# Two ways to end a gated-experts kernel: tails for the whole last unit, or pairs and rows closed inside it

## The chip, the cores and the metric

The kernel runs on one core of a Trainium2 chip. The metric is the device time of one execution in microseconds (us); lower is better. A core has TensorE (matrix products, into the PSUM banks), VectorE, ScalarE and GpSimd (called PE, DVE, ACT and POOL in the profile), and SyncE (SP), which issues most of the transfers (DMAs).

## What is computed

`x` holds 8 items of 512 positions by 256 channels, all in float32. Eight experts and a shared one have weights of 256 by 1024 (gate, up) and 1024 by 256 (down).

```python
g = einsum('bsd,edf->ebsf', h, Wg)
u = einsum('bsd,edf->ebsf', h, Wu)
expert_outs = einsum('ebsf,efd->ebsd', silu(g) * u, Wd)
expert_output = einsum('be,ebsd->bsd', gating_probs, expert_outs)
shared = einsum('bsf,fd->bsd', silu(h @ Sg) * (h @ Su), Sd)
sg = shared_gate_prob[:, :, None]
out = x + (1.0 - sg) * expert_output + sg * shared
```

## The kernel before

The work is cut into 36 **units**: two halves of four items, nine experts, and two groups of four blocks of 128 hidden columns. A unit multiplies four items j by four blocks i, gate and up (m = 0 and 1), which gives sixteen tiles h[i, j] of 128 by 512, and multiplies these with the down weights. Both products are done with fewer multiplications than the plain ones, by sums and differences of operands: the diagonal i = j first (the *hub*: `P_step`, `Q_step`), then six **pairs** (i, j) of `PAIRS` (line 66), each with the two off-diagonal tiles (`R1_step`, `R_step`, lines 534 to 553). One "product" here is 128x128 by 128x512 and shows as two matmul records in the profile.

Each bank goes the same way. For r = 1 VectorE adds D (line 552); for m = 0 ScalarE applies Silu (line 477); for m = 1 VectorE multiplies gate, coefficient and up into h (line 482). Before a pair, ScalarE **seeds** a bank by copying an earlier difference into it (line 532), and the pair's product accumulates on that. The operands of a pair are V and b (sums of x) and U and W (sums of weights); in unit 0 they are computed (`x_difference` line 319, `x_sums` lines 334 and 335, `w_difference` 417, `w_sums` 427 to 430) and V, b are stored to DRAM, from where later units load them (lines 324, 341).

The **down projection** of a unit is `down` (line 587), 26 products, run while the next products of gate and up are running: it starts at the unit's step 22 (`TAKE`) and ends in the next unit. Per pair there are three products: `first` (r), `second` (S or s) and the product of X = h[j, i] - h[i, j] (line 674). Then for each i come p_i (sums of rows, with accumulator b_i) and q_i (sums of columns, with accumulator B_i). GpSimd makes the row and column sums (line 577). The accumulators stay in SBUF over all units of a half; `carried` copies one into a bank with ScalarE (line 615), multiplies, and copies it back (line 624); `put` adds a bank to an accumulator with VectorE (lines 603 to 607). There are two banks for all this (`new_po`), used in turn.

A half must be **closed** (`closes`): in its last unit each pair adds its accumulator V to the bank (line 678) and puts the sum into b_i and b_j, and each row i puts p_i into B_i. The closed b_i and B_i are a transposed output.

The order on TensorE and GpSimd is written by hand and is the program's order; ScalarE's too in unit 0. It comes from strings (lines 874 to 878): G is one step of gate and up, D one of down, T one of turning x, X one tail. On the other queues the framework's scheduler puts the instructions in order; `issue_after` (line 123) makes one instruction stand behind another in its queue, without a semaphore. `BEHIND` (line 300) is a table of such pairs for unit 0.

The **last unit** (n = 35) is different. Its down projection is not done by pairs: each of its 32 `tail` steps (line 763) multiplies a half of h[i, j] with the plain down weights, four records of 128x128 by 128x256, straight into rows of the output. So the accumulators of the second half are closed one unit earlier, in unit 34, whose down ends in the hub of unit 35. There `END_STEPS` (line 886) lists, by the number of G steps done: "turn" transposes b_i and B_i of a row (line 739), "store" sends them in eight DMAs to a DRAM scratch (issued at line 953, one for each G), "load" brings them back as rows in two DMAs (line 757), "x" loads the rows of x, "add" adds both on GpSimd (line 761). When a tail group is complete, `store_rows` (line 775) adds it to those rows on VectorE and stores them to the output.

Of the kernel before, what the change touches and what calls it, by code (L numbers as in the profile page):

```python
# [17 lines left out]
def kernel(  # L18
# [40 lines left out]
    P = 128  # L59
# [5 lines left out]
    CI = (0.0, 1.0, -1.0, 2.0)  # L65
    PAIRS = ((1, 0), (0, 2), (3, 0), (1, 2), (3, 1), (3, 2))

    OWN = (0, 1, 2, 3)
# [71 lines left out]
    xdram = {}  # L140
    recent = {}


# [152 lines left out]
    def load_x(h, i):  # L296
# [4 lines left out]
        ("b", 0): ("x", 2), ("v", 1): ("P", 2), ("h", 2): ("P", 3), ("v", 2): ("other", 0, 1),  # L301
        ("b", 1): ("v", 2), ("h", 3): ("v", 2), ("v", 3): ("X", 0), ("v", 4): ("X", 1), ("v", 5): ("X", 2),
    }
# [170 lines left out]
    def finish(u, m, i, j, bank):  # L474
        if m == 0:
            s = spool.tile([P, S], F32, tag="sg", name=f"sg{i}{j}_{u.name}")
            nc.scalar.activation(s, bank, AF.Silu)  # L477
            u.sg[i, j] = s
        else:
            b = NI * u.h + j  # L480
            t = hpool.tile([P, S], F32, tag="h", name=f"h{i}{j}_{u.name}")
            made = ve.scalar_tensor_tensor(  # L482
                t, u.sg[i, j], coef[:, u.e, b : b + 1], bank, ALU.mult, ALU.mult
            )
            if i == j:
                first_order(u, made, "h", i)
            u.h_[i, j] = t
# [56 lines left out]
    def R_step(u, p, m, r):  # L544
        i, j = PAIRS[p] if r == 0 else PAIRS[p][::-1]
        bank = u.bank[i, j, m]
        nc.tensor.matmul(  # L547
            bank, u.W[p][:, r, m], u.VB[p][:, r],
            start=False, stop=True, skip_group_check=True,
        )  # L550
        if r == 1:
            ve.tensor_add(bank, bank, u.Ds[j, m])  # L552
        finish(u, m, i, j, bank)


    def h_sums(u, p):


        i, j = PAIRS[p]
        if u.n + 1 == len(units):  # L560
            return
        u.X[p] = tpool.tile([P, S], F32, tag="t", name=f"X{p}_{u.name}")
        made = (gp if closes(u) and p in (1, 2, 3, 4) else ve).tensor_tensor(  # L563
            u.X[p], u.h_[j, i], u.h_[i, j], ALU.subtract
        )
        first_order(u, made, "X", p)
        for k, l in ((i, j), (j, i)):
            for which, n in (("rows", k), ("cols", l)):
                u.sums.append((which, n, (k, l)))
# [12 lines left out]

    def closes(u):

        return u.n + (2 if u.h + 1 == NH else 1) == len(units) * (u.h + 1) // NH

    def down(u, acc):
# [54 lines left out]
        def pair(p):  # L642
# [8 lines left out]
            def second():  # L651
                args = u.Wd[p][j], u.h_[j, i]
                if p in OWN and not closes(u):
                    carried(("S", p), *args)
                    return
# [8 lines left out]

            if closes(u) and p < SWAPPED:
                second()
                yield
                A, k = first()
            else:
                A, k = first()  # L670
                yield
                second()
# [3 lines left out]
            )  # L676
            if closes(u):
                ve.tensor_add(A, A, acc["V", p])
                put(("b", i), A, 1.0 / d)
                put(("b", j), A, -1.0 / d)  # L680
            else:
                put(("V", p), A, 1.0)
# [4 lines left out]
        done = {}  # L687
        for what in (0, 1, 2, 3, 4, "p0", "q0", 5, "q1", "p1", "q2", "p2", "q3", "p3"):
            if isinstance(what, int):
# [14 lines left out]
            else:  # L704
# [3 lines left out]
                done[what] = po  # L708
            if closes(u) and f"p{i}" in done and f"q{i}" in done:
                if CI[i] != 0.0:  # L710
# [7 lines left out]
    def turn_back(h, i, r):  # L718
# [5 lines left out]
        if (i, 1 - r) not in BACK[BACK.index((i, r)):]:  # L724
            for q in range(4):
                outgoing.append((squares(out, NI * h + i, q), t[ts(q, 32)]))

    last_rows = {}
    tails = {}
    ended = {}  # L730
    end_rows = {}

    def end_step(kind, i):

        b = NI * (NH - 1) + i
        if kind == "turn":
            t = iopool.tile([P, 2, S], F32, tag="io", name=f"end{i}")
            for r in range(2):
                ve.transpose(t[:, r], ends.pop((NH - 1, i, r)))
            ended[i] = t  # L740
        elif kind == "store":
            to = end_rows[i] = dram.tile([S, D], F32, tag=f"end{i}", name=f"endrows{i}")
            at = to.rearrange("(c r t) d -> r t c d", r=32, t=NT)
            for r in range(2):
                for q in range(4):
                    outgoing.append((
                        at[:, :, :, ts(4 * r + q, 32)],
                        ended[i][ts(q, 32), r].rearrange("r (t c d) -> r t c d", t=NT, d=32),
                    ))
        elif kind == "x":  # L750
            last_rows[i] = load_rows(xpool, "x", b)
        elif kind == "load":
            at = end_rows[i].rearrange("(p t) d -> p t d", t=NT)
            end_rows[i] = []
            for c in range(2):
                t = sumpool.tile([P, 2, D], F32, tag="sum", name=f"endin{i}_{c}")
                nc.sync.dma_start(t, at[:, 2 * c : 2 * c + 2])
                end_rows[i].append(t)
# [4 lines left out]
    def tail(u, i, j, c):  # L763

        first = (j, c) not in tails
        if first:
            pool, tag = (ps_g, f"g{c}") if j == 2 else (ps_o, f"po{c}")
            tails[j, c] = pool.tile([P, 2, D], F32, tag=tag, name=f"tail{j}_{c}")
# [6 lines left out]
    def store_rows(j, c):  # L775
        b = NI * (NH - 1) + j
        xr = last_rows[j][c]
        for t in (0, 1) if j == NI - 1 and c == 1 else (slice(0, 2),):
            ve.tensor_add(xr[:, t], tails[j, c][:, t], xr[:, t])
            at = out[b].rearrange("(p c t) d -> p c t d", c=2, t=2)[:, c]  # L780
            nc.sync.dma_start(at[:, t], xr[:, t])

# [8 lines left out]
    def gate_up(u, nxt):  # L791
# [5 lines left out]
        def sums(p):  # L797
            x_sums(u, p)
            w_sums(u, p)

        for p, make in ((0, w_difference), (0, w_sums), (1, w_difference), (1, w_sums)):
            make(u, p)
        if u.n:
            make_at(u, 3)
        w_difference(u, 2)
        ahead = ((0, x_difference), (0, x_sums), (1, x_difference), (1, x_sums), (2, x_difference))
        if u.n:
# [3 lines left out]
        for kind, i, m in hub_steps(u):  # L811
# [17 lines left out]
            at = range(10, 16) if u.n in LATE_FORMS else range(3, 14, 2)  # L829
            if step == at[0] - 1 and u.n and nxt is not None:  # L830
                make_ad(u)
            if step in at and u.n and nxt is not None:
                d_forms(u, at.index(step))
            yield
        if u.n == 0:
            make_ad(u)
            for p in range(len(PAIRS)):
                d_forms(u, p)
        for p in range(len(PAIRS)):
            last = p + 1 == len(PAIRS)  # L840
            if p + 3 < len(PAIRS):
                (differences if u.n else partial(w_difference, u))(p + 3)
            if nxt is not None:
                if p >= 2:
                    load_w(nxt, p - 2)
                    if p < 5:
                        make_at(nxt, p - 2)
            store_forms(u)
            if p == 5 and nxt is not None:
                load_d(nxt)  # L850
            if not last and u.n:
                seed(u, p + 1)
            for m in range(2):
                if not last and (u.n or p or m):
                    R1_step(u, p + 1, m)
                elif last and nxt is not None:
# [3 lines left out]
                for r in range(2):  # L860
                    R_step(u, p, m, r)
                    if m == 1 and r == 1:
                        h_sums(u, p)
                        if u.n == 0 and p + 2 < len(PAIRS):
                            seed(u, p + 2)
                        if p + 2 < len(PAIRS):
                            sums(p + 2)
                        if u.n == 0 and p < 2:
                            x_difference(u, p + 3)
                    if u.n == 0 and (p, m, r) == (3, 0, 1):  # L870
                        x_difference(u, 5)
# [5 lines left out]
    FIRST = "TGGTGGTGG" + "G" * 16 + BLOCK * 5  # L877
    LAST = HUB + BLOCK + "GGXGGXGGX" * 5 + "X" * 17
    TAILS = [
        tuple(int(n) for n in what)  # L880
        for what in (
            "000 100 001 101 200 201 300 301 110 111 010 011 210 211 310 311 "
            "220 020 120 221 021 121 330 030 130 331 031 131 320 321 230 231"
        ).split()
    ]
    END_STEPS = {
        7: (("turn", 0), ("store", 0)), 16: (("turn", 1), ("store", 1)), 18: (("x", 0),),
        20: (("turn", 2), ("store", 2), ("x", 1)), 22: (("load", 0), ("x", 2)),
        24: (("turn", 3), ("store", 3), ("x", 3)), 28: (("add", 0),), 30: (("load", 1),),
        34: (("add", 1),), 37: (("load", 2),), 40: (("add", 2),), 44: (("load", 3),),  # L890
        47: (("add", 3),),
    }

    for i in range(NI):
# [37 lines left out]
    for u in units:  # L932
# [6 lines left out]
        for what in FIRST if u.n == 0 else LAST if nxt is None else ORDER:  # L939
            if what == "G":  # L940
                if nG == TAKE:
                    for _ in behind:
                        pass
                    if u.opens:
                        acc = {}
                    behind = down(u, acc) if nxt is not None else iter(())
                if final and nxt is not None and nG in (18, 21, 24, 27):
                    load_x(u.h + 1, (nG - 18) // 3)
                if nxt is None:
                    for what_, i in END_STEPS.get(nG, ()):  # L950
                        end_step(what_, i)
                if outgoing:
                    nc.sync.dma_start(*outgoing.pop(0))
                if nG > TAKE and nG % 2 == 0 and u.sums:
                    add_sum(u)
# [5 lines left out]
            elif what == "T":  # L961
                for _ in range(2):
                    next(turning, None)
            elif what == "X":
                i, j, c = TAILS.pop(0)
                tail(u, i, j, c)
# [56 lines left out]
```

## Time and profile before

| | |
|---|---|
| median of 3 runs | 2434.99 us (2433.91 to 2435.68) |
| the profiled execution | 2433.26 us, span 2431.5 us, TensorE's clock 1.000 |
| TensorE busy in the first 20 us, the next 20, the last 11.5 | 18.51, 19.44, 7.70 us |
| TensorE's waits, by releaser | 1.2 us for a memset at the start, 0.8 for ScalarE's seed (line 532, twice), 0.3 for VectorE (line 208) |
| SP's waits for VectorE's finished rows (line 781) | 26.1 us, 7 times |
| tails (line 770) | 128 records, 379 ns each |

A line of the timeline reads: start in us from the beginning of the span, duration, engine, line, operation, what it writes <- what it reads (tile names without numbers), shape, and how many records were merged; in brackets the idle time before it and what released it. Matmul records overlap: the busy time of one is 592 ns, but the next starts before it ends, so the distance between starts is what counts. A row of DMA issues ends with the size of one and the median time from issue to landing.

### The profile page before, as it was taken

Reading aid. Unit: us, or ns where it says so; the run is one execution under the profiler, and the core shown is the slowest. Engines: PE = TensorE matmul, PEld = TensorE weight load, DVE = VectorE, ACT = ScalarE, POOL = GpSimd, SP = SyncE. Lnnn points to the kernel's source line nnn. Section 1 sums busy time; section 2 is a strip of 40 time slices with the busy share of each in tenths; the row PEclk is TensorE's granted clock in tenths of the full one; section 3 lists DMA queues with packets and bytes.
Section 4 is the critical chain, followed back from the end, with each engine's and each line's share of the span. In section 5 each row is a group of like instructions: output and inputs, shape, how many; then the busy total and the mean of one; then the engine's idle time right before and its main releaser. Section 6 shows DMA issues by size and latency. Waiting matters only on the chain.

```text
span 2431.5 us, 22779 instructions
## 1 busy us (share of the span) xinstructions
PE 2425.3 (100%) x5736; PEld 1085.0 (45%) x5736; DVE 1918.3 (79%) x2861; ACT 1240.0 (51%) x2294; POOL 2085.3 (86%) x2321
## 2 busy tenths in 40 slices
PE   9999999999999999999999999999999999999999
PEld 4444444444444444444444444444444444444446
DVE  7788878778787877787887777777877777777795
ACT  5555454554555555555455555555455555555542
POOL 8988888898988989898888888888888888888882
PEclk9999999999999999999999999999999999999999
DMA  4333333334333333334353323323333333233245
GB/s 150 114 110 111 107 95 103 119 117 125 105 120 105 101 113 94 109 113 124 119 122 112 91 83 91 92 87 90 100 104 104 95 99 91 87 89 93 83 133 140
DMA packets 221201, 257.92 MB, mean 106 GB/s; under 512 B 64016, under 2 KB 156432, under 8 KB 221072
## 3 DMA queue, kind: packets, MB, share of 16 engines
q1 hardware_dynamic: 220240, 256.17, 35.7%
q8 instruction: 48, 0.79, 0.1%
q14 instruction: 81, 0.66, 0.1%
q10 hardware_dynamic: 832, 0.30, 0.0%
HBM read 238.59 MB, written 17.83 MB: 105 GB/s over the span
## 4 chain that ended last, share of the span: by engine, by line
PE 99%; DVE 1%; issue 0%; ACT 0%; DVEq 0%
PE c L547 30%; PE c L537 15%; PE c L515 10%; PE c L493 10%; PE r L639 7%; PE r L674 7%; PE b L616 5%; PE S L616 5%; PE q L639 5%; PE s L639 2%; PE tail L770 1%; PE B L616 0%; DVE h L482 0%; DVE c L542 0%; DVE c L552 0%
## 5 line engine op out<-in xcount | busy, mean ns | idle before, releaser
L547 PE MATMUL c<-b,wb 128*128 128x512 f32 x1728 | 847.2, 592 | 0.0
L477 ACT ACTIVATE sg<-c 128x512 f32<-128x512 f32 x576 | 343.8, 597 | 574.4 <-DVE c L552 332.4
L482 DVE SCALAR_TENSOR_TENSOR h<-sg,coef,c 128x512 f32<-128x512 f32 x576 | 427.4, 742 | 242.2 <-PE c L547 134.8
L547 PEld LDWEIGHTS c<-b,wb 128*128 128x128 f32 x1728 | 328.2, 190 | 409.2 <-issue 388.7
L537 PE MATMUL c<-v,u 128*128 128x512 f32 x864 | 441.1, 593 | 0.8 <-ACT c L532 0.8
L577 POOL TENSOR_TENSOR rows<-rows,h 128x512 f32<-128x512 f32 x280 | 369.3, 1319 | 0.0
L542 DVE TENSOR_TENSOR c<-D,c 128x512 f32<-128x512 f32 x432 | 298.7, 692 | 78.1 <-ACT sg L477 59.3
L577 POOL TENSOR_TENSOR cols<-cols,h 128x512 f32<-128x512 f32 x280 | 358.4, 1280 | 0.0
L552 DVE TENSOR_TENSOR c<-c,D 128x512 f32<-128x512 f32 x432 | 298.5, 691 | 21.2 <-PE c L547 20.7
L493 PE MATMUL c<-x,w 128*128 128x512 f32 x572 | 274.5, 592 | 0.0
L429 POOL TENSOR_TENSOR wb<-u,wb 128x256 f32<-128x256 f32 x108 | 78.8, 730 | 221.4 <-ACT wb L427 221.4
L537 PEld LDWEIGHTS c<-v,u 128*128 128x128 f32 x864 | 163.4, 190 | 207.9 <-issue 167.7
L674 PE MATMUL r<-X,ud 128*128 128x512 f32 x420 | 214.5, 592 | 0.0
L639 PE MATMUL r<-h,wd 128*128 128x512 f32 x420 | 214.5, 592 | 0.0
L515 PE MATMUL c<-x,at 128*128 128x512 f32 x432 | 208.5, 592 | 0.0
L525 ACT COPY D<-c 128x512 f32<-128x512 f32 x284 | 165.7, 584 | 81.4 <-DVE h L482 81.3
L563 DVE TENSOR_TENSOR X<-h,h 128x512 f32<-128x512 f32 x202 | 198.1, 981 | 6.8
L577 POOL TENSOR_TENSOR rows<-h,h 128x512 f32<-128x512 f32 x140 | 195.1, 1394 | 0.0
L577 POOL TENSOR_TENSOR cols<-h,h 128x512 f32<-128x512 f32 x140 | 180.6, 1290 | 0.0
L499 ACT COPY P<-c 128x512 f32<-128x512 f32 x216 | 126.4, 587 | 106.1 <-PE c L493 101.5
L493 PEld LDWEIGHTS c<-x,w 128*128 128x128 f32 x572 | 108.5, 190 | 135.9 <-issue 111.7
L615 ACT COPY S<-accS 128x512 f32<-128x512 f32 x132 | 77.8, 590 | 157.5 <-DVE accV L603 140.7
(115 smaller groups left out, 3473.6 us busy)
## 6 DMA issues: line engine op xcount, KB each, us to landing
b<-xs SPq DMA_DIRECT2D x210, 512.0 KB, 3.6
v<-xs SPq DMA_DIRECT2D x210, 256.0 KB, 2.6
wd<-in_L_cond_Wd_dram SPq DMA_DIRECT2D x32, 512.0 KB, 4.9
w<-in_L_cond_Wg_dram SPq DMA_DIRECT2D x127, 128.0 KB, 3.5
w<-in_L_cond_Wu_dram SPq DMA_DIRECT2D x127, 128.0 KB, 3.6
f<-xd SPq DMA_DIRECT2D x12, 512.0 KB, 5.2
xs<-f SPq DMA_DIRECT2D x18, 256.0 KB, 2.9
xin<-in_x_dram SPq DMA_DIRECT2D x16, 256.0 KB, 4.4
```

What stands on the lines that cost most here:

```text
L477: nc.scalar.activation(s, bank, AF.Silu)
L482: made = ve.scalar_tensor_tensor(t, u.sg[i, j], coef[:, u.e, b : b + 1], bank, ALU.mult, ALU.mult)
L493: nc.tensor.matmul(bank, u.raw[i][:, m, 0], xhub[u.h, i][:, 0], start=True, stop=True)
L515: nc.tensor.matmul(bank, u.at[i][:, m], xhub[u.h, i][:, 1], start=False, stop=True, skip_group_check=True,)
L537: nc.tensor.matmul(bank, u.U[p][:, m], u.V[p], start=False, stop=True, skip_group_check=True)
L542: first_order(u, ve.tensor_sub(other, u.Ds[j, m], bank), "other", p, m)
L547: nc.tensor.matmul(bank, u.W[p][:, r, m], u.VB[p][:, r], start=False, stop=True, skip_group_check=True,)
L552: ve.tensor_add(bank, bank, u.Ds[j, m])
L577: gp.tensor_tensor(sums[n], u.h_[n, n] if first else sums[n], u.h_[at], ALU.add)
L616: nc.tensor.matmul(po, w, b, start=not full, stop=True, skip_group_check=full)
L639: nc.tensor.matmul(po, w, b, start=True, stop=True)
L674: nc.tensor.matmul(A, u.Ud[p], u.X[p], start=False, stop=True, skip_group_check=True)
```

## The change

In the last unit, pairs 0, 1 and 3 of `PAIRS`, which are (1, 0), (0, 2) and (1, 2), are kept as pairs with their three down products each, and rows 0, 1 and 2 get their p and q. These pairs and rows are closed in unit 35; pairs 2, 4, 5 and row 3 are closed in unit 34 as before. Only the tails with a 3 in them stay, 14 of 32. The pairs of the last unit run in the order 0, 1, 3, 2, 4, 5. Its string is written anew, so are `TAILS` and `END_STEPS`; rows 1 and 2 get their last steps when twelve tails are left, with `issue_after` for each group of stores and loads. Six of the eight stores of row 2 go to ScalarE's queue, its transposed tiles come from another pool.

Besides, five places of the order of issue: in unit 0 the sum b of pair 1 and the second bank of pair 1 stand behind the add (line 552) of pair 0, `w_sums` comes before `x_sums`, and `x_difference` of pair 5 comes one step earlier; in closings the add of V (line 678) stands behind the h that was made last.

```diff
+    LAST_PAIRS = (0, 1, 3)
+    LAST_ROWS = (0, 1, 2)
...
-        ("b", 1): ("v", 2), ("h", 3): ("v", 2), ("v", 3): ("X", 0), ("v", 4): ("X", 1), ("v", 5): ("X", 2),
+        ("b", 1): ("add", 0, 0), ("other", 1, 0): ("add", 0, 0), ("h", 3): ("v", 2), ("v", 3): ("X", 0), ("v", 4): ("X", 1), ("v", 5): ("X", 2),
...
-            nc.scalar.activation(s, bank, AF.Silu)
+            u.last_silu = nc.scalar.activation(s, bank, AF.Silu)
...
+            latest_h[:] = u, made
...
-            ve.tensor_add(bank, bank, u.Ds[j, m])
+            first_order(u, ve.tensor_add(bank, bank, u.Ds[j, m]), "add", p, m)
...
-        if u.n + 1 == len(units):
+        if p not in pairs_of(u):
             return
...
+    def closes(u, p=None, i=None):
+
+        if u.h + 1 < NH:
+            return u.closes
+        if (p in LAST_PAIRS) if i is None else (i in LAST_ROWS):
+            return is_last(u)
+        return u.n + 2 == len(units)
...
-            if closes(u):
-                ve.tensor_add(A, A, acc["V", p])
+            if closes(u, p):
+                made = ve.tensor_add(A, A, acc["V", p])
+                if latest_h[0] is u:
+                    issue_after(made, latest_h[1])
                 put(("b", i), A, 1.0 / d)
                 put(("b", j), A, -1.0 / d)
...
-        for what in (0, 1, 2, 3, 4, "p0", "q0", 5, "q1", "p1", "q2", "p2", "q3", "p3"):
+        order = (0, 1, 2, 3, 4, "p0", "q0", 5, "q1", "p1", "q2", "p2", "q3", "p3")
+        for what in (0, 1, "p0", "q0", 3, "q1", "p1", "q2", "p2") if is_last(u) else order:
...
+                    queue = nc.scalar if i == 2 and 4 * r + q < 6 else nc.sync
...
+                if i in LAST_ROWS:
+                    issue_after(made, recent["b"])
+                latest_rows[:] = [made]
+                if i in (1, 2):
+                    issue_after(made, closing_stores[2, nc.sync][-1])
...
-            x_sums(u, p)
-            w_sums(u, p)
-
+            for make in (x_sums, w_sums) if u.n else (w_sums, x_sums):
+                make(u, p)
...
-                    if u.n == 0 and (p, m, r) == (3, 0, 1):
+                    if u.n == 0 and (p, m, r) == (3, 0, 0):
                         x_difference(u, 5)
...
-    LAST = HUB + BLOCK + "GGXGGXGGX" * 5 + "X" * 17
+    LAST = HUB + BLOCK * 3 + "GDGDGGDGDGD" + "GDDGDDGGGG" + "GGGXGGGXX" + "X" * 11
...
-            "000 100 001 101 200 201 300 301 110 111 010 011 210 211 310 311 "
-            "220 020 120 221 021 121 330 030 130 331 031 131 320 321 230 231"
+            "330 331 030 031 300 301 310 311 130 131 230 231 320 321"
...
+        18: (("x", 0),), 20: (("x", 1),), 22: (("x", 2),),
+        24: (("turn", 3), ("store", 3), ("x", 3)), 34: (("load", 3),),
+        39: (("turn", 0), ("store", 0)), 42: (("turn", 1), ("store", 1)),
+        43: (("turn", 2), ("store", 2), ("load", 0)), 46: (("add", 3), ("add", 0)),
     }
+    LAST_STEPS = (("load", 1), ("load", 2), ("add", 1), ("add", 2))
...
+                if len(TAILS) == 12:
+                    for made in closing_stores[0, nc.sync][4:]:
+                        issue_after(made, recent["b"])
+                    for made in closing_stores[1, nc.sync]:
+                        issue_after(made, *latest_rows)
+                    for made in closing_stores[2, nc.scalar]:
+                        issue_after(made, u.last_silu)
+                    for made in closing_stores[2, nc.sync]:
+                        issue_after(made, *closing_stores[1, nc.sync])
+                    for what_, i in LAST_STEPS:
+                        end_step(what_, i)
```

## The prediction

> **What bounds the kernel now.** I read the page first: busy shares and the chain that ended last.
>
> ```profile
> PE 2425.3 (100%) x5736; PEld 1085.0 (45%) x5736; DVE 1918.3 (79%) x2861; ACT 1240.0 (51%) x2294; POOL 2085.3 (86%) x2321
> PE 99%; DVE 1%; issue 0%; ACT 0%; DVEq 0%
> ```
>
> TensorE is the bound from the first product to the last, at a granted clock of 1.000. Only two things can change the time: the number of products, and holes in TensorE's row. So I looked for holes in the timeline of TensorE. One 128x128 by 128x512 product is two matmul records; their starts lie 0.43 us apart, so a product is 0.86 us of pace. In the first unit the pace breaks at three places:
>
> ```profile
> 27.98 1.88 PE L547 MATMUL c<-b,wb 128*128 128x512 f32 x4
> 30.40 1.13 PE L537 MATMUL c<-v,u 128*128 128x512 f32 x2 [0.54 <-ACT c L532]
> ...
> 38.23 1.02 PE L537 MATMUL c<-v,u 128*128 128x512 f32 x2
> 39.27 1.12 PE L547 MATMUL c<-b,wb 128*128 128x512 f32 x2
> ...
> 53.11 1.02 PE L674 MATMUL r<-X,ud 128*128 128x512 f32 x2
> 54.42 1.10 PE L537 MATMUL c<-v,u 128*128 128x512 f32 x2 [0.30 <-ACT c L532]
> ```
>
> Four records from 27.98 should hand over at 29.70; the next starts at 30.40. After each hole the following record is another 0.1 late. The holes are 0.8, 0.3 and 0.5 us. The next are in the closing of each half. This is the second half's:
>
> ```profile
> 2315.14 1.02 PE L674 MATMUL r<-X,ud 128*128 128x512 f32 x2
> 2316.00 1.02 PE L537 MATMUL c<-v,u 128*128 128x512 f32 x2
> 2316.86 1.02 PE L547 MATMUL c<-b,wb 128*128 128x512 f32 x2
> 2317.93 1.12 PE L616 MATMUL S<-h,wd 128*128 128x512 f32 x2
> ```
>
> The S product should start at 2317.72. VectorE over the same time says why it waits:
>
> ```profile
> 2316.54 0.69 DVE L678 TENSOR_TENSOR r<-r,accV 128x512 f32<-128x512 f32 x1
> 2317.14 0.73 DVE L482 SCALAR_TENSOR_TENSOR h<-sg,coef,c 128x512 f32<-128x512 f32 x1
> 2317.79 0.68 DVE L603 TENSOR_TENSOR accb<-r,accb 128x512 f32<-128x512 f32 x1
> ```
>
> The closing add stands ahead of the h that S reads; h ends at 2317.87. The hole is 0.2 plus 0.1 us, and the first half has the same one at 1178.5 to 1179.1. Both halves show another 0.3 us in the next unit's hub (1227 to 1229, 2366 to 2368). Everything between is full: 1000.00 us busy in a window of 1000 us.
>
> Then the end:
>
> ```profile
> 2425.93 3.16 SPq L781 DMA_DIRECT2D out_dram<-xin  x5
> 2427.80 0.76 DVE L779 TENSOR_TENSOR xin<-tail,xin 128x256 f32<-128x256 f32 x2 [0.17 <-PE tail L770]
> ```
>
> TensorE's last record starts at 2427.32; the additions and the last store take the span to 2431.5. The profiled run is 2433.26 us, 1.73 below the median of the runs, 2434.99.
>
> **Part 1, fewer products.** Before, the last unit's down projection is 32 tail steps, each four 128x256 records, 0.86 us. After, 14 tails stay, and the three kept pairs add 3 x 3 products, their three rows and three columns 6. 14 + 15 = 29, three products less: 3 x 0.86 = **2.6 us**, all on the bound engine.
>
> **Part 2, the first unit.** Hole 1: ScalarE's seed copy (29.76) follows a Silu (29.13) that waited for VectorE's add at L552 (28.41). TensorE finished that add's product by 27.3, but VectorE ran the sum b of pair 1 (27.02, 0.87) and another bank (27.81, 0.68) first. Both go behind the add now, which can start at 27.32; the seed ends at 29.2 and the hole is gone. What is late next: VectorE runs without a break from 23.9 to 35.2, and the reorder takes no work off it. Its v of pair 3 (33.47 to 34.68) starts a chain of six ScalarE instructions up to the seed that ends at 37.78; TensorE asks for that seed at 38.23 before and would ask at 37.4 after. So of 0.8 us about 0.35 survive. Hole 2: the product at 39.27 waits for POOL's L429, 38.49 to 39.22, behind a 1.27 us POOL sum at 37.26. With weights first, L429 ends at 37.99; POOL's sum comes 1.45 us later, ends at 40.0, and is read by the product at 40.5. The hole closes (0.3). Hole 3: ScalarE at 52.20 runs Silu, then a multiply of v (0.5), then a copy, then the seed. The multiply goes ahead of the Silu, into 1.2 us of its idle time, so the seed ends about 0.5 earlier; VectorE's 0.26 us of waiting at 44.5 gives some too. Total after the third hole: between 0.35 (the waits only move) and 1.6 (all three close); I take **0.9**, the sum of what VectorE's unbroken stretch lets through.
>
> **Part 3, the closing add behind h.** The S product no longer waits in the first half: 0.3 us. In the second half pairs 0 and 1 don't close there any more, which leaves ordinary order: 0.3 us. Behind the add stand two updates of accumulators, 0.6 us each, whose readers come products later. Total **0.6**. The holes in the hubs stay: they are Silu, copy and seed behind one product, and nothing edits that.
>
> **Part 4, what the last unit must now close.** Here the change adds waits, and TensorE's order is written by hand, so it blocks. Product p0 is seeded from accumulator b0, and b0 gets its last term from X of pair 1, with one product (0.86) between X and p0. The path from X: h (0.65, now forced ahead), closing add (0.6), b0 (0.6), ScalarE's copy (0.6), p0. The nearest row is the old closing of pair 5: X starts at 2359.23, the copy it releases ends at 2363.66, 4.43 us, with a foreign add (0.75) and a second accumulator (0.6) in it. Less these, 3.1, and with h ahead 3.7; X and one product cover 1.72. Stall: 1.4 to 2.0, I take 1.8. Product p1 comes two products after X of pair 3 and reuses the bank in which X was summed, so both accumulators must be written first: by counting 4.0, by the row 4.43, less 2.58 covered: 1.5 to 1.9, and 3.1 should the transposes of row 0 get ahead on VectorE; I take 1.6, near the row. Queued behind these on TensorE is everything that remains; nothing takes it back. Below nothing isn't possible for either: the sum before had no such pair of products and no hole there. Sum **+3.4**. ScalarE (51%) and POOL have room: POOL idles 9.76 us at 2366 and 5.70 at 2378, and takes on 12 sums of 1.3, two X and the forms of three pairs.
>
> **Part 5, the rows at the end.** Rows 0, 1, 2 are now turned, stored, loaded and added behind p2. From the end of p2 there are 22 products, 18.9 us. The longest way is row 2: six of its eight stores wait on ScalarE's queue for the last Silu, six products later, 6.7 us with its add; then six issues. The rows for these are:
>
> ```profile
> endrows<-end SPq DMA_DIRECT2D x32, 64.0 KB, 3.1
> endin<-endrows SPq DMA_DIRECT2D x8, 256.0 KB, 4.0
> ```
>
> An issue is 0.616 (median of the 32), so the stores are out at 10.4 and landed at 13.5; load issue 0.4, landing 4.0 at the median, 3.55 for the last one before, where it is quiet; then two POOL additions of 1.27. That ends at 19.5 to 20.0; the last product is ready at 19.1. The Trainium skill ("DMA: Bandwidth & Descriptors", [...]Issuing engines are not separate DMA queues) says that a second queue saves only the time to initiate, "usually small relative to the DMA itself". Here the issue row, six times 0.62, is as long as a landing, so on SP these would cost 3.7 us more; but on ScalarE they also wait for the Silu. I keep to the rows: **+0.4**, with 0 by the shortest landings (2.1, 3.0) and +3 by the longest (4.6, 4.7).
>
> **Sum:** -2.6 - 0.9 - 0.6 + 3.4 + 0.4 = -0.3. 2433.26 - 0.3 = 2433.0 for a profiled run; on the median, 2434.99 - 0.3 = **2434.7**. About 0.2% (4.9 us) is what a measurement of this kernel can tell from no change: 2430.1 to 2439.9.
>
> **Rivals.** *The saving is kept*: the seeds of p0 and p1 come in time because VectorE reached its adds early, and the end is hidden: -2.6 - 0.9 - 0.6 = -4.1, 2430.9; with all first-unit holes closed 2430.2. For it: VectorE has gaps of 0.4 to 1.9 us in the last unit before. Against: p0 hangs on a path of four dependent instructions that one product can't cover. *The closing ends late*, the slower side: SP takes row 0's eight stores, load 0, row 1's eight stores and the loads one behind the other, each load standing until its stores land. By the rows, load 1 goes out 12 us after p2 if VectorE turns row 0 six us before p2. VectorE has 24 us of work in the 23 us from X of pair 1 on (11.5 for the banks and h of three pairs, 14 accumulator updates at 0.6, six transposes at 0.67). From 4 us of lateness on, load 1 lands at 20, POOL's four additions (5.1) follow, and the end is some 6 us behind TensorE: -0.7 + 6 = 2440.3. *The first unit only moves its waits* and hubs or pairs gain nothing: -2.6 - 0.6 + 3.8 + 0.4, 2436.
>
> **How the numbers follow.** Forecast (2433 to 2437) 0.58; saving kept (2430.2 to 2433) 0.25; waits moved 0.07; late closing 0.10. Faster by over 0.2% needs everything: 0.04. Slower is the late closing nearly whole: 0.09. Same 0.87. The range leaves out the end of each rival: 2431 to 2438.
>
> **What would show it.** TensorE with 5694 records (5736 - 128 + 14 x 4 + 15 x 2). No hole at 29.7 and 39.1, a smaller one near 37.4 or 53. No S hole at 1178 and 2317. In the last unit a hole of 1.5 to 2 us ahead of a b product (L616), twice. At the end, POOL's last addition within 1 us of TensorE's last product. If there is no hole in the last unit, part 4 is wrong; if the last additions wait for a load by several us, part 5 is.

## The result, and the profile after

The changed kernel is slower. Its median is 2445.19 us (2442.23 to 2447.68, 6 runs), against 2435.34 for the kernel before, run beside it: +9.9 us, a ratio of 1.0038 (95% interval 1.0028 to 1.0049). The range on record, 2431 to 2438, does not hold it.

The profiled run took 2443.51 us, 10.25 more than the profiled run of before, with 5694 matmul records, as forecast. The page's busy shares and chain:

```profile
PE 2426.4 (99%) x5694; PEld 1077.6 (44%) x5694; DVE 1926.5 (79%) x2873; ACT 1246.2 (51%) x2306; POOL 2105.1 (86%) x2344
PE 96%; DVE 2%; POOL 1%; issue 0%; ACT 0%; DMA 0%; ACTq 0%; POOLq 0%; DVEq 0%; SPq 0%
```

TensorE is busy 1.1 us longer with 42 records fewer, and the chain leaves it for 4% of the span instead of 1%: the time went into holes. (Line numbers are those of the changed kernel: L552 was L547, L542 was L537, L633 was L616, L691 was L674, L557 was L552, L656 was L639, L486 was L482, L582 was L577.) The timeline of TensorE in the first unit:

```profile
28.10 1.88 PE L552 MATMUL c<-b,wb 128*128 128x512 f32 x4
29.81 1.02 PE L542 MATMUL c<-v,u 128*128 128x512 f32 x2
...
36.68 1.06 PE L691 MATMUL r<-X,ud 128*128 128x512 f32 x2
38.18 1.10 PE L542 MATMUL c<-v,u 128*128 128x512 f32 x2 [0.43 <-ACT c L537]
39.11 1.02 PE L552 MATMUL c<-b,wb 128*128 128x512 f32 x2
...
52.84 1.02 PE L691 MATMUL r<-X,ud 128*128 128x512 f32 x2
54.12 1.10 PE L542 MATMUL c<-v,u 128*128 128x512 f32 x2 [0.25 <-ACT c L537]
```

The hole at 29.7 is gone (29.81 follows 28.10 at the pace). It came back one pair later, at 38.18, as the prediction said it might; the one at 39.1 closed, the one at 53.7 stayed at 0.4. In unit 35, the last, TensorE's timeline shows what made most of the loss:

```profile
2366.00 1.96 PE L520 MATMUL c<-x,at 128*128 128x512 f32 x4
2369.80 1.13 PE L656 MATMUL q<-cols,ad 128*128 128x512 f32 x2 [1.84 <-POOL cols L582]
...
2383.64 1.88 PE L552 MATMUL c<-b,wb 128*128 128x512 f32 x4
2386.48 1.13 PE L691 MATMUL r<-X,ud 128*128 128x512 f32 x2 [0.96 <-ACT sg L481]
...
2395.47 1.02 PE L542 MATMUL c<-v,u 128*128 128x512 f32 x2
2398.85 2.04 PE L633 MATMUL b<-rows,wd 128*128 128x512 f32 x2 [2.37 <-ACT b L632]
2400.69 1.64 PE L552 MATMUL c<-b,wb 128*128 128x512 f32 x2
...
2410.28 1.02 PE L656 MATMUL q<-cols,ad 128*128 128x512 f32 x2
2413.90 1.12 PE L633 MATMUL b<-rows,wd 128*128 128x512 f32 x2 [2.60 <-ACT b L632]
```

The b products at 2398.85 and 2413.90 are p0 and p1. Summing what every distance between two starts has beyond the pace gives, in us (the numbers in the table are these sums, not the idle times in brackets):

| hole | before | after |
|---|---|---|
| first unit | 1.8 | 1.5 |
| closing of the first half | 0.65 | 0.63 |
| unit 34 | 0.3 | 1.25 |
| unit 35: hub, q waits for GpSimd | 0.3 | 2.2 |
| unit 35: X of pair 0, X of pair 3 | - | 1.5, 0.4 |
| unit 35: p0, then four records at half speed | - | 2.5, 1.6 |
| unit 35: p1, p2 | - | 2.9, 0.6 |

That is 12.0 us more; three products less give 2.6 back; TensorE's last record starts at 2436.76 instead of 2427.32 (+9.4). The span ends 4.9 us behind that start instead of 4.2 (+0.8). Together 10.2.

### The profile page after: what moved, and what is told of

The parts are those of the page before. It is cut to its first block, busy times and chain, and to the rows that moved or that the text cites. A ratio compares the mean times of both kernels' runs of the same rounds, so it can differ in the third digit from the quotient of the medians.

```text
span 2441.7 us, 22735 instructions
## 1 busy us (share of the span) xinstructions
PE 2426.4 (99%) x5694; PEld 1077.6 (44%) x5694; DVE 1926.5 (79%) x2873; ACT 1246.2 (51%) x2306; POOL 2105.1 (86%) x2344
## 4 chain that ended last, share of the span: by engine, by line
PE 96%; DVE 2%; POOL 1%; issue 0%; ACT 0%; DMA 0%; ACTq 0%; POOLq 0%; DVEq 0%; SPq 0%
PE c L552 29%; PE c L542 15%; PE c L520 10%; PE c L498 10%; PE r L656 7%; PE r L691 7%; PE b L633 5%; PE S L633 5%; PE q L656 5%; PE s L656 2%; DVE h L486 0%; DVE c L557 0%; POOL cols L582 0%; POOL rows L582 0%; PE B L633 0%
## 5 line engine op out<-in xcount | busy, mean ns | idle before, releaser
L552 PE MATMUL c<-b,wb 128*128 128x512 f32 x1728 | 847.6, 593 | 0.0
L486 DVE SCALAR_TENSOR_TENSOR h<-sg,coef,c 128x512 f32<-128x512 f32 x576 | 427.2, 742 | 241.2 <-PE c L552 130.8
L552 PEld LDWEIGHTS c<-b,wb 128*128 128x128 f32 x1728 | 328.6, 190 | 413.6 <-issue 393.7
L542 PE MATMUL c<-v,u 128*128 128x512 f32 x864 | 441.1, 593 | 0.7 <-ACT c L537 0.7
L582 POOL TENSOR_TENSOR rows<-rows,h 128x512 f32<-128x512 f32 x283 | 373.1, 1318 | 0.0
L582 POOL TENSOR_TENSOR cols<-cols,h 128x512 f32<-128x512 f32 x283 | 361.8, 1278 | 0.0
L547 DVE TENSOR_TENSOR c<-D,c 128x512 f32<-128x512 f32 x432 | 298.5, 692 | 78.7 <-ACT sg L481 59.5
L557 DVE TENSOR_TENSOR c<-c,D 128x512 f32<-128x512 f32 x432 | 298.4, 691 | 18.8 <-PE c L552 18.5
L542 PEld LDWEIGHTS c<-v,u 128*128 128x128 f32 x864 | 163.5, 190 | 209.0 <-issue 166.4
L691 PE MATMUL r<-X,ud 128*128 128x512 f32 x426 | 217.8, 593 | 1.1 <-ACT sg L481 1.0
L656 PE MATMUL r<-h,wd 128*128 128x512 f32 x426 | 217.7, 592 | 0.0
L582 POOL TENSOR_TENSOR rows<-h,h 128x512 f32<-128x512 f32 x143 | 198.9, 1391 | 0.0
L582 POOL TENSOR_TENSOR cols<-h,h 128x512 f32<-128x512 f32 x143 | 184.6, 1291 | 0.0
```

The source lines that it names most:

```text
L486: made = ve.scalar_tensor_tensor(t, u.sg[i, j], coef[:, u.e, b : b + 1], bank, ALU.mult, ALU.mult)
L542: nc.tensor.matmul(bank, u.U[p][:, m], u.V[p], start=False, stop=True, skip_group_check=True)
L547: first_order(u, ve.tensor_sub(other, u.Ds[j, m], bank), "other", p, m)
L552: nc.tensor.matmul(bank, u.W[p][:, r, m], u.VB[p][:, r], start=False, stop=True, skip_group_check=True,)
L557: first_order(u, ve.tensor_add(bank, bank, u.Ds[j, m]), "add", p, m)
L582: gp.tensor_tensor(sums[n], u.h_[n, n] if first else sums[n], u.h_[at], ALU.add)
```

## The experiments

**Theory:** TensorE's order, written by hand, asks for products of unit 35 before VectorE, ScalarE or GpSimd can have fed them. **Rivals:** the rows' way to the end (turn, store, load, add) sets the time; or the first-unit edits cost it. Medians, with the kernel before run beside each set:

| run | median us | before | ratio (95%) |
|---|---|---|---|
| e1, the five places alone | 2434.42 | 2435.54 | 0.9995 (0.9987 to 1.0004) |
| e12, the same again | 2434.02 | 2435.42 | 0.9994 (0.9985 to 1.0002) |
| e2, late forms | 2443.28 | 2435.54 | 1.0029 (1.0017 to 1.0040) |
| e3, p not seeded | 2444.12 | 2435.54 | 1.0033 (1.0021 to 1.0046) |
| e4, row 3 turned later | 2444.84 | 2435.54 | 1.0039 (1.0027 to 1.0052) |
| e5, e2 and pair 3 ahead of p0 | 2441.98 | 2435.24 | 1.0026 (1.0015 to 1.0037) |
| e6, e5 with loads behind all stores | 2442.16 | 2435.24 | 1.0027 (1.0018 to 1.0036) |
| e7, e6 with a shared addition and stores 4 and 4 | 2444.84 | 2435.24 | 1.0036 (1.0024 to 1.0049) |
| e8, row 2 on one queue | 2444.33 | 2436.14 | 1.0035 (1.0022 to 1.0049) |
| e9, no way for rows 0 to 2 | 2446.34 | 2436.14 | 1.0043 (1.0030 to 1.0056) |
| e10, e5 without that way | 2436.83 | 2436.14 | 1.0005 (0.9997 to 1.0013) |
| e11, e5 with another order on SyncE | 2441.56 | 2436.14 | 1.0023 (1.0013 to 1.0033) |

The reference beside the sets moves between 2435.24 and 2436.14, and the first unit's holes differ between profiles of the same code by up to 1.9 us (1.5 to 3.4). So a difference of one or two us between two rows says little alone; below it is read together with the hole that the run was made to close.

**e1 and e12: the kernel before with the five places only** (the first-unit and closing lines of the diff above).

> The old last unit with the five places of issue order alone. Theory (the loss sits in units 34 and 35, where TensorE's written order asks for products too early): the first unit's holes shrink by some 0.3 us as in the changed kernel and the S hole of the closings goes or moves, so 0 to 1 us faster than before (2434.5 to 2435.3). Rival (the new order of issue costs in itself): slower than before by 2 us or more.

> The old last unit with the five places of issue order alone, a second time, since its first interval (0.9987 to 1.0004) did not settle whether it beats the kernel before. If the 1.1 us of the first time are real: a ratio of 0.9993 to 0.9998 again. If they were chance: 1.000 or above.

Medians 1.1 and 1.4 us below the kernel before; both intervals still hold 1. The five places do not cost the 10 us, so that rival falls; whether they gain stays open, though both lean that way. The two profiles do not show where it would come from: their first units have 3.1 and 1.9 us of holes, where the kernel before had 1.8. It is the one version here that does all the work and does not lose.

**e2: forms later in the last hub.**

```diff
-    LATE_FORMS = (1, len(units) // NH, len(units) // NH + 1)
+    LATE_FORMS = (1, len(units) // NH, len(units) // NH + 1, len(units) - 1)
```

> The changed kernel, with the down forms of the last unit made late in its hub (steps 10 to 15, as after the first half's closing) instead of between the sums of unit 34. Theory: the hole of 2.0 us ahead of product q at 2369.8, which waits for GpSimd's column sum, goes; 1.5 to 2.2 us faster than the changed kernel, 2443 to 2443.7. Rival (the rows' chain through SyncE's stores and loads sets the end): the hole goes and the time stays within 0.5 us of 2445.2.

1.9 us faster than the changed kernel, by the medians. Of the hub's 2.2 us of holes 0.6 are left (0.3 in the kernel before). GpSimd's timeline of the changed kernel shows what the hole was:

```profile
2367.26 0.46 POOL L461 TENSOR_TENSOR ud<-ad 128x128 f32<-128x128 f32 x1
2367.80 0.72 POOL L466 TENSOR_TENSOR wd<-ud,a 128x256 f32<-128x256 f32 x1
2368.48 1.26 POOL L582 TENSOR_TENSOR cols<-cols,h 128x512 f32<-128x512 f32 x1
```

The column sum that q waits for ends at 2369.74. The new forms of three pairs (`ud`, `wd`; the last is shown) and `make_ad` stand ahead of it in GpSimd's written order.

**e3: p0, p1, p2 not seeded.** This run leaves something out: B takes the last product of p alone, where the kernel takes the whole closed b.

```diff
+            elif what[0] == "p" and is_last(u):
+                flush_sums(u, "rows", i)
+                po, _ = single(("b", i), u.raw_d[:, i, 0:P], u.rows[i])
+                put(("b", i), po, 1.0)
+                done[what] = po
```

> The changed kernel, with p0, p1 and p2 of the last unit not seeded from their accumulators: the products start in an empty bank and VectorE adds it to b afterwards. Theory: the hole of 2.5 us ahead of p0 goes with the four half-speed records behind it (1.7 us), that ahead of p1 (2.8) shrinks to 1 to 2 us because the bank is still to be freed; 4 to 6 us faster than the changed kernel, 2439.5 to 2441. Rival (the rows' chain sets the end): the holes go, TensorE ends earlier, and the last additions of GpSimd come 4 us or more behind it; time within 1 us of 2445.

p0's hole goes, 0.8 us are left (at q0); p1's is 2.1 us and waits for VectorE to have read the bank, not for a seed. TensorE's last record starts 2.7 us earlier (2434.09), but the median is only 1.1 lower, not the 4 to 6 expected: the end now comes 6.8 us behind that record. So the theory and the first rival each hold a part.

**e4: row 3 turned five steps later.**

```diff
-        24: (("turn", 3), ("store", 3), ("x", 3)), 34: (("load", 3),),
+        24: (("x", 3),), 29: (("turn", 3), ("store", 3)), 37: (("load", 3),),
```

> The changed kernel, with the turning and storing of row 3 five steps later (its load three steps later). Theory: the 1.1 us hole ahead of X of pair 0 (2386.5), which waits for an accumulator update behind two transposes on VectorE, goes; but VectorE is full until 2398, so part comes back ahead of p0: 0 to 1.5 us faster than the changed kernel, 2443.7 to 2445.2. Rival (the rows' chain sets the end): 0.5 us or more slower, since row 3's stores now stand ahead of row 0's.

Nothing that can be told from noise was gained (-0.35). The hole ahead of X of pair 0 is halved (from 1.1 to 0.5), p0's grows from 2.5 to 2.7, and X of pair 1 gets a new one of 0.2: VectorE is full there (5.97 of the 6 us from 2394), so part of the hole moved on with the work. The profile also loses 1.7 us to half-speed records behind q which the changed kernel's does not.

**e5: pair 3 ahead of p0.** With e2's line:

```diff
-        for what in (0, 1, "p0", "q0", 3, "q1", "p1", "q2", "p2") if is_last(u) else order:
+        for what in (0, 1, 3, "p0", "q0", "q1", "p1", "q2", "p2") if is_last(u) else order:
...
-        39: (("turn", 0), ("store", 0)),
+        40: (("turn", 0), ("store", 0)),
```

> The changed kernel with the late forms of the run before, and with pair 3 of the last unit done ahead of p0 and q0 (the order 0, 1, 3, p0, q0, q1, p1, q2, p2; row 0 is turned one step later). Each p then comes five or more products after the X that its accumulator waits for, and the bank that p1 takes has been free longer. Theory (products asked too early): the holes of 2.5 us ahead of p0 and 2.8 us ahead of p1 go, and TensorE's last record starts 5 us earlier than with the late forms alone, near 2429.5. How much of it the time shows tells the rival (the rows' chain through SyncE sets the end) apart: if TensorE alone counts, 2438 to 2439; if the chain counts, the time stays at 2441 to 2443 and the last additions of GpSimd come 4 us or more after TensorE's last record.

The holes of p0 and p1 are 0 and 0.9 us now. TensorE's last record starts at 2431.70, 2.7 us earlier than in e2, in spite of a first unit with 1.9 us more holes than in the changed kernel's profile. The time falls by 1.3 us only. The end of e5, all engines (without the weight loads):

```profile
2423.71 8.37 PE L810 MATMUL tail<-wd,h 128*128 128x256 f32 x38
...
2428.55 2.10 SPq L792 DMA_DIRECT2D endin<-endrows  x4
...
2434.09 2.49 POOL L801 TENSOR_TENSOR xin<-xin,endin 128x512 f32<-128x512 f32 x2 [0.20 <-DMA endin<-endrows]
2436.62 0.76 DVE L819 TENSOR_TENSOR xin<-tail,xin 128x256 f32<-128x256 f32 x2 [0.20 <-POOL xin L801]
```

The last additions wait for GpSimd, GpSimd for loads that SyncE could issue only at 2428.55. The span ends 9.2 us behind TensorE's last start, where it was 4.2 in the kernel before. So the rows' way is a second wall, 5 us further out, which the holes had hidden.

**e9 and e10: the walls apart.** The stores, loads and additions of rows 0 to 2 are left out, of the changed kernel and of e5.

```diff
+        if i in LAST_ROWS and kind in ("store", "load", "add"):
+            return
...
```

> The changed kernel without the way of rows 0, 1 and 2 behind their turning: their stores to the scratch, loads and additions are left out, so those rows lack the accumulators. What remains is TensorE's order with its holes. If TensorE's holes alone set the changed kernel's time: its end comes 4.2 us after TensorE's last record as before, 0.5 to 1.5 us faster than the changed kernel, 2443.7 to 2444.7. If the rows' chain sets it: 3 us faster or more.

> The run with pair 3 ahead of p0 (2442.0), again without the stores, loads and additions of rows 0, 1 and 2. If its end is set by the rows' chain, as its trace reads (last additions 5 us after TensorE's last record), it gains 4 to 6 us: 2436 to 2438. If TensorE sets it: within 1 us of 2442.

e9 is not faster than the changed kernel (2446.3 against 2445.2), though 0.5 to 1.5 us had been expected. Its span ends 4.2 us behind TensorE's last start instead of 4.9, so the rows' way cost the changed kernel's profile some 0.7 us; this profile's first unit happens to have 1.7 us more holes. TensorE's order set that time. e10 is 5.2 us faster than e5: there the rows' way set it. In e10 the last additions follow TensorE (compare the last line with e5's):

```profile
2429.87 0.76 DVE L821 TENSOR_TENSOR xin<-tail,xin 128x256 f32<-128x256 f32 x2 [0.17 <-PE tail L812]
```

Even so e10 is no faster than the kernel before: 1.25 us of holes in unit 34 and 4.6 in unit 35 remain, 5.2 more than before, and three products are worth 2.6.

**e6, e7, e8, e11: the queues.** e6 sends the loads of rows 0, 1, 2 behind all stores; e7 also gives row 1's addition to VectorE and parks four stores on ScalarE's queue instead of six (parked: they stand there behind the last Silu and go out after it); e8 is the changed kernel with none parked; e11 is e5 with none parked and the order stores 0, stores 1, load 0, stores 2, loads 1 and 2. Shown are the lines in which they differ most; e6, e7 and e11 also have e5's lines, and e7 has e6's.

```diff
e6  -    LAST_STEPS = (("load", 1), ("load", 2), ("add", 1), ("add", 2))
e6  +    LAST_STEPS = (("load", 0), ("load", 1), ("load", 2), ("add", 0), ("add", 1), ("add", 2))
...
e7  -                gp.tensor_tensor(xr, xr, t, ALU.add)
e7  +                (ve if i == 1 else gp).tensor_tensor(xr, xr, t, ALU.add)
e7  -                    queue = nc.scalar if i == 2 and 4 * r + q < 6 else nc.sync
e7  +                    queue = nc.scalar if i == 2 and 4 * r + q < 4 else nc.sync
e8  -                    queue = nc.scalar if i == 2 and 4 * r + q < 6 else nc.sync
e8  +                    queue = nc.sync
...
e11 -        43: (("turn", 2), ("store", 2), ("load", 0)), 46: (("add", 3), ("add", 0)),
e11 +        43: (("load", 0), ("turn", 2), ("store", 2)), 46: (("add", 3), ("add", 0)),
...
```

> The run before with the loads of rows 0, 1 and 2 on SyncE's queue behind the stores of all three, so that no store waits for a landing: row 1's stores no longer stand behind the load of row 0. If the rows' chain counts: 1 to 3 us faster than the run before. If TensorE alone counts: the same within 0.5 us.

> The run before with row 1's addition on VectorE instead of GpSimd, and row 2's stores split four and four between ScalarE's and SyncE's queues instead of six and two. If the rows' chain counts: GpSimd has two additions of 1.25 us less in it and row 2 lands about 1 us earlier, 1 to 2.5 us faster than the run before. If TensorE alone counts: the same within 0.5 us.

> The changed kernel with all eight stores of row 2 on SyncE's queue, none on ScalarE's. If the second queue only saves time to issue, this is slower: six issues of 0.62 us more on SyncE, up to 3.7 us. If the six stores parked behind the last Silu held back SyncE's (the trace shows SyncE's last store standing 4.0 us for a landing of the same tensor, and in every run of the study SyncE's stores stop while ScalarE's go out), it costs nothing: within 1 us of 2445.2.

> A version meant to be better: the run with pair 3 ahead of p0, all stores on SyncE, in the order rows 0 and 1, load of row 0 (landed by then), row 2, loads of rows 1 and 2. If the chain is what its parked stores and its waiting loads make it: 1.5 to 3 us faster than 2442.0, and still slower than the kernel before, since GpSimd's six additions (7.5 us) and SyncE's 24 stores (15 us at 0.62) stay.

e6 and e11 gain nothing that the intervals resolve, and e7 loses 2.7 us against e6. All three were to gain if the rows' way sets the end. e8 costs nothing, as expected of parked stores that hold others back. The longest wait of SyncE's queue in the changed kernel, 2415 to 2432:

```profile
SPq L759 <- DMA endrows<-end: 4.0, 1, 4.0
```

In the compiled programs the reason can be read: the DMAs of both queues take turns on eight semaphores, and each waits until the one that had its semaphore before has landed. The trace agrees: SyncE's last store goes out at 2428.05, and the store on ScalarE's queue that had the same semaphore landed at 2428.03. A store parked on ScalarE's queue behind the last Silu keeps its semaphore, and SyncE's store that comes after it on that semaphore stands still. In e7 SyncE stops from 2417.6 to 2421.6 in the middle of row 1, until the first of the four parked stores has landed (2421.50). In e11 no store is parked, but the chain keeps its length: 16 stores take 11.5 us, the rest of stores and loads lasts until 2429.7, and GpSimd's additions run to 2435.3.

## Why the prediction was wrong

The steps that failed are the last unit's closings (part 4) and the closing add (part 3). The sum on record was -0.3, the profiles lie 10.2 apart. Of these 10.5 us, 6.0 are waits in the last unit that the sum had at nothing, 2.0 are p0 and p1 mis-sized, 1.5 are the closing add, 0.6 the first unit and 0.4 the rows.

**Fewer products:** right, 5694 records.

**The first unit (-0.9):** the mechanism held, the size did not. The first hole closed and returned at VectorE's v of pair 3, as written, but with 0.7 us where 0.35 was to survive. The second closed. The third kept its 0.5: its seed ends 0.3 us earlier, and TensorE asks for it 0.3 earlier. Together 0.3 us came out between the two profiles. The profiles with this same first unit show holes of 1.5 to 3.4 us in sum, the large ones with one of 1.6 to 1.75 that begins at 54.5. In e5 VectorE's X and v run 1.67 and 1.75 us beside GpSimd's sums instead of the 0.99 and 1.21 of the changed kernel's profile. One profile could not carry 0.9.

**The closing add (-0.6):** failed. In the first half the hole moved one pair on (1197, still 0.3): two updates of b now hold the bank that r needs, so their readers do not come "products later". In unit 34, "which leaves ordinary order" was the step that failed. Pairs 1 and 3 no longer close there, so nothing puts the next h first, and their update of V stands ahead of it. S of pair 2 and s of pair 4 read that h and wait, 0.4 and 0.3 us; S of pair 3, which is seeded now, waits 0.5 for a bank that two updates of b hold. In e1 and e12, with the same closing add but with all pairs closing in unit 34, its holes are 0.3 us. The lines for S of pair 2 and S of pair 3:

```profile
2324.09 0.68 DVE L620 TENSOR_TENSOR accV<-r,accV 128x512 f32<-128x512 f32 x1
2324.68 0.74 DVE L486 SCALAR_TENSOR_TENSOR h<-sg,coef,c 128x512 f32<-128x512 f32 x1
2325.57 1.10 PE L633 MATMUL S<-h,wd 128*128 128x512 f32 x2
...
2335.74 0.59 ACT L632 COPY S<-accS 128x512 f32<-128x512 f32 x1 [1.43 <-DVE accb L624]
2336.38 1.13 PE L633 MATMUL S<-h,wd 128*128 128x512 f32 x2 [0.28 <-ACT S L632]
```

**The last unit's closings (+3.4):** the two places were right, and mis-sized. VectorE and ScalarE behind X of pair 1 (2394.61):

```profile
2395.42 0.69 DVE L547 TENSOR_TENSOR c<-D,c 128x512 f32<-128x512 f32 x1
2396.01 0.74 DVE L486 SCALAR_TENSOR_TENSOR h<-sg,coef,c 128x512 f32<-128x512 f32 x1
2396.67 0.69 DVE L695 TENSOR_TENSOR r<-r,accV 128x512 f32<-128x512 f32 x1
2397.39 0.69 DVE L620 TENSOR_TENSOR accb<-r,accb 128x512 f32<-128x512 f32 x1
2398.12 0.59 ACT L632 COPY b<-accb 128x512 f32<-128x512 f32 x1 [0.74 <-DVE accb L620]
```

The path is the one on record, with a foreign bank (2395.42) ahead of h, the kind of instruction that the working had taken out of the old row: from X to p0 4.24 us instead of 3.7, a hole of 2.5 instead of 1.8. For p1, behind X of pair 3 (2408.49):

```profile
2410.34 0.69 DVE L695 TENSOR_TENSOR r<-r,accV 128x512 f32<-128x512 f32 x1
2411.34 0.69 DVE L620 TENSOR_TENSOR accB<-q,accB 128x512 f32<-128x512 f32 x1 [0.31 <-PE q L656]
2411.95 1.28 DVE L624 SCALAR_TENSOR_TENSOR accb<-r,accb 128x512 f32<-128x512 f32 x2
2413.26 0.59 ACT L632 COPY b<-accb 128x512 f32<-128x512 f32 x1 [2.21 <-DVE accb L624]
```

VectorE waited for q1 and took it in before the two b's: 5.41 us instead of 4.2, a hole of 2.9 (with the 0.1 by which the next record is late) instead of 1.6. Missing altogether were 6.3 us, 0.3 of which stood there before: GpSimd's order in the hub (2.2), X of pairs 0 and 3 (1.5 and 0.4), p2 (0.6), and the slow records behind p0's hole (1.6). X of pair 0 adds its product to a bank that VectorE must have read first, and that read stands behind the two transposes of row 3. (The bracket above names ScalarE's Silu, but in e4 the same X starts 0.6 us after that Silu and 0.06 after VectorE's read.)

```profile
2383.96 0.70 DVE L773 STREAM_TRANSPOSE end<-accb 128x512 f32<-128x512 f32 x1
2384.59 0.66 DVE L773 STREAM_TRANSPOSE end<-accB 128x512 f32<-128x512 f32 x1
...
2385.76 0.67 DVE L620 TENSOR_TENSOR accB<-r,accB 128x512 f32<-128x512 f32 x1
```

"POOL idles 9.76 us at 2366 [...] and takes on [...] the forms" was the wrong reading: idle time later in the unit does not help a sum that stands behind the forms in a written order. e2 shows that for the hub: with the forms later, 1.6 of its 2.2 us go.

**The rows (+0.4):** near in size, 0.8 measured, but by luck: TensorE had been delayed as well, and where it is not (e5) the rows end 5 us too late. The rival "closing ends late" named the right chain, load 1 standing for SyncE's stores, and gave 2440.3. It did not set the time of the changed kernel (e9). It is the wall at 2441 to 2442 when the holes are closed (e5, e11), and without it the time is 2436.8 (e10). I priced it from an issue of 0.62 and left out that a DMA also waits for the one that had its semaphore before it.

What stays open: how much the five places gain (e1, e12), and the holes of unit 34 and of X of pair 0 one by one. Their causes are read from the traces, and no run closed one of them alone.

## What to carry to other kernels

Where one engine's order is written by hand, count for each new product not only the work but the path from its last input, through every engine's queue in its order, and compare it with the products between. A saving of three products (2.6 us) was used up by one such path here (2.5 us for p0, 2.9 for p1). When a hole is closed, ask which chain was waiting behind it: closing 4 us of holes in unit 35 (8.6 to 4.6, from e2 to e5) gave 1.3, since the rows' chain stood right behind. A second queue gained nothing here while its transfers were parked, because they kept semaphores that the first queue needed.

## What the runs showed that was not expected

TensorE's granted clock fell behind some holes. By stages of the changed kernel (window, length, busy time of PE, PEld, DVE, ACT and POOL, clock, DMA share, GB/s):

```profile
2394.00:2398.00 4.00, 2.49 (x6) 0.76 (x4) 3.90 (x6) 1.10 (x2) 4.00 (x4) 1.00 0.54 148
2398.00:2400.00 2.00, 1.15 (x2) 0.66 (x3) 0.68 (x2) 0.59 (x1) 2.00 (x4) 0.63 0.60 227
2400.00:2402.00 2.00, 2.00 (x4) 0.85 (x3) 0.45 (x1) 1.03 (x2) 2.00 (x2) 0.52 0.00 0
```

Records start 0.85 us apart instead of 0.43, four of them, and 1.6 us are lost. It followed six of the sixteen holes of 2.0 to 2.8 us in the last unit of the changed kernel, e2, e3, e4, e8 and e9: four times of five behind p0, never in e2. The Trainium skill ("TensorE: Matmul & The Clock Gate", What's actually happening) says that the clock halves after an idle window of some 3.4 us that runs free of the kernel. The half rate agrees; the holes here are shorter than the window, and the same hole did it in one profile and not in another.

The traces show more. Each of these six half-rate stretches lasted 3.41 us, and every full-rate stretch is a whole number of 3.413 us long (the shorter ones are 23.89, 27.31 and 37.55 us: 7, 8 and 11 of them). So the clock changes only at the lines of a grid of 3.413 us, and a hole that such a line cuts counts in two parts. All five grid steps that held more than 2.1 us of a hole were followed by a step at half rate, one of three that held 2.0 was, and none that held 1.94 or less. In e2 a line cut p0's hole into 1.6 and 0.9 us. So some 60% of a step idle were enough, and where the lines fell in the hole differed from profile to profile.
